# Cross-attention on one core: turned probabilities and y fetched back by quarters of the rows instead of quarters of the keys

## The chip, the cores and the metric

The kernel runs on one NeuronCore of one Trainium2 chip. The metric is the device time of one execution in microseconds (us). A core has a matrix engine (PE, with weight loads shown as PEld), a vector engine (DVE), a scalar engine (ACT), GpSimd (POOL) and a sequencer for transfers (SP). Transfers between HBM and the on-chip memory of 128 partitions are issued on SP's queue here, apart from the loads of the four last text rows and the gathered accumulations, which POOL issues. The profile speaks of the core's 16 DMA engines, which carry out all of them.

## The reference

One layer of cross-attention over `x` (2 x 2048 x 640, f32) with 128 text rows of width 384, 8 heads of 80. The last 4 text rows are the "adapter" rows.

```python
query = hidden_states @ Wq
hs = _mha(query, enc @ Wk, enc @ Wv)              # softmax over 124 text keys
ca_q1 = einsum('btc,th->bch', ca, Wq_ca)[:, indices, :]
ca_hs1 = _mha(ca_q1, residual, residual)          # adapter: the 2048 rows of x are keys and values
ca_hs2 = _mha(ca_hs1 @ Wq, ca @ Wk_ca, ca @ Wv_ca)
out = (hs + ca_hs2) @ Wout + b_out + residual
```

`indices` picks 2048 places out of 384 columns, so only 384 rows of the adapter branch are distinct; the kernel computes these and gathers them for the output rows.

## The kernel before

**Order of work.** A planner (`Desk`, from line 65) replays generators, each of which yields pieces of work with the events that they wait for, the buffers that they need and free, and a rank. It keeps an estimated clock per engine and records, one piece at a time, the one that can start first on its estimate. The order on each engine is therefore fixed when the program is built, and every engine works through its own list in that order. A transfer is recorded by `Desk.dma` (line 263) on SP's list; the number that follows its two sides is only the planner's estimate of its time. When the program runs, an engine waits on semaphores for what its next instruction needs. The transfers of SP go round eight semaphores in turn, so that a transfer is also issued only after the one eight places earlier on SP's list has landed.

**Text branch.** The 2 x 2048 rows are treated as 16 units `m` of two tiles of 128 rows. `text_scores` puts a tile's scores (128 rows x 8 heads x 124 keys) into PSUM, `softmax` turns them into probabilities, and a DVE transposition of 32 x 32 blocks writes them into the single buffer `eb` as `[128, 4, 8, 32]`: partition `32 i + b` is key place `b` of row block `i`, the second index `j` is the quarter of the keys (32 keys each). One transfer of 512 KB carries `eb` to a scratch tensor `kept` in HBM (128 x 4 x 2 x 256 values for both tiles of a unit); `eb` is free when that transfer has landed. This is needed because the block transposition leaves the 32 keys of every quarter on the partitions of their row block, while the product with the values wants all 128 keys on the partitions.

`probabilities` (line 2017) brings a unit back into `pT`, `[128, 4, 2, 8, 32]`: partition `32 j + b` is the key, the second index `i` the row block. It issues four transfers of 256 KB each. There are two `pT` buffers, and the transfers wait for both `kept` transfers of the unit and for the buffer. After that, `residual` (line 2107) issues the loads of the unit's rows of `x` into `x_more` or `last_rows`, `hidden` (line 2144) multiplies `vpad` by `pT` into `ph` (48 matmuls a unit), ACT or DVE copies `ph` to `hs`, and PE multiplies by sums of columns of `Wout` into `po` (`text_out_fast`, line 2171). DVE adds `po` to the loaded rows of `x`, POOL adds the adapter's result by a gathered, accumulating transfer (`add_second`), and SP stores the tile.

**Adapter branch.** For each of two batches `b` and four blocks `sb` of 512 rows, `yz_block` makes `yz` on PE. `y_rows` (line 1609) turns its y part by 32 x 32 blocks on DVE into `yt`, sends it to a scratch tensor in HBM by two transfers, and fetches it back into `y_sb` by four transfers of 128 KB. The z part becomes `zop`; for the second batch it goes to HBM and comes back as `zb`. `s` is the product of `zop` and `cop`, `ea` its exponential on ACT, and `contract` multiplies `ea` by `y_sb[:, sb, g]` into `acc`, for `g` from 0 to 3. The blocks of the second batch overwrite those of the first, so their fetch waits for the first batch's `acc`.

**Queries.** `pq` is made in blocks of 512 rows. What of its split into high and low parts is needed by the scores goes to HBM as `away` and returns as `landing`, which ACT casts to `rests`; the second half of a tile's scores (`sc<-krest,rests`) waits for that.

Of the kernel before, what the change touches and what calls it, by code (L numbers as in the profile page):

```python
# [64 lines left out]
class Desk:  # L65
# [197 lines left out]
    def dma(self, out, in_, us, issue=0.45, more=2.8):  # L263

        self.pin(self.nc.sync.dma_start(out, in_))
        self.spent += issue
        self.channel = max(self.channel, self.now + self.spent) + us
        self.landed = self.channel + more
# [3 lines left out]
def kernel(  # L272
# [29 lines left out]
    R = D2 - P  # L302
# [11 lines left out]
    matmul, transpose, copy, dma = desk.matmul, desk.transpose, desk.copy, desk.dma  # L314
# [94 lines left out]
    y_sb = const.tile([P, NSB, 4, 2, 4, G], F32, name="y_sb")  # L409
# [1119 lines left out]
    def yz_block(b, sb):  # L1529
# [24 lines left out]
        for u in range(2):  # L1554
            yield Do(
                "ACT", lambda u=u: desk.a_activation(yz[:, u, :], pyz[u], AF.Identity, bias=ones),
                [op.at], frees=[(banks, s[u])], marks=[("yz", b, sb, u)],
            )
        yield Fork(y_rows(b, sb), 9)
        away = hbm.tile([P, 2, 512], F32, tag=f"z_{sb}", name=f"z_{b}_{sb}") if b else None  # L1560
        if not b:
# [47 lines left out]
    def y_rows(b, sb):  # L1609

        yz = yz_of[b, sb]
        kept = hbm.tile([P, 4, 2, 4 * G], F32, tag=f"y_{b}_{sb}", name=f"y_{b}_{sb}")
        for u in range(2):

            def turn(z, u=u):
                t = late["pool"].tile([P, 512], F32, tag=f"yt{z[0]}", name=f"yt_{b}_{sb}_{u}")
                desk.v_transpose(
                    t.rearrange("p (a s k) -> p a s k", a=4, s=4),
                    yz[:, u, :].rearrange("p (s a t) -> p a s t", s=4, a=4),
                )  # L1620
                return t

            op = yield Do("DVE", turn, [("yz", b, sb, u), "late"], needs=[(yts, 1)], rank=0.5)

            def away(t=op.value, u=u):
                dma(kept[:, :, u, :], t.rearrange("p (a n) -> p a n", a=4), 1.0)

            yield Do("SP", away, frees=[(yts, op.slots[0][0])], marks=[("y out", b, sb, u)], rank=0.5)
        both = [("y out", b, sb, u) for u in range(2)]
        yield Do(  # L1630
            "NONE", lambda: None, [("zop", b, sb, u, "away") if b else ("zop", b, sb, u) for u in range(2)] + both,
            frees=[(yzs, 0)],
        )
        yield Do("NONE", lambda: None, both + ([("acc done", b - 1, u) for u in range(2)] if b else []))
        by_tokens = kept.rearrange("(g t) a u n -> a t g (u n)", g=4)
        for a in range(4):

            def back(a=a):
                dma(
                    y_sb[R * a : R * (a + 1), sb].rearrange("p g u s k -> p g (u s k)"),  # L1640
                    by_tokens[a], 0.4,
                )

            op = yield Do("SP", back, rank=0.5, marks=[("y", b, sb, a)])

    def adapter(b):

# [369 lines left out]
    def probabilities(m):  # L2017

        yield Do("NONE", lambda: None, [("kept", m, 0), ("kept", m, 1)])
        kept = kept_of[m].rearrange("p j k n -> p j (k n)")  # L2020
        by_keys = kept.rearrange("(i b) j n -> j b i n", i=4)
        op = yield Do(
            "NONE", lambda z: wide("pT", z[0], f"pT_{m}"), needs=[(pTs, 1)], marks=[("back", m)],
        )
        room_of["pT", m] = op.slots[0][0]
        pT = op.value
        for j in range(4):
            op = yield Do(
                "SP",
                lambda: dma(pT[R * j : R * (j + 1)].rearrange("p i k h a -> p i (k h a)"), by_keys[j], 1.1),  # L2030
                [("kept", m, 0), ("kept", m, 1)], rank=0,
            )
        pT_of[m] = pT
        desk.event(("pT", m)).t = op.at.t
        yield from text_out(m)
# [3 lines left out]
    def wide(kind, i, name):  # L2039

        if i == SPARE:
            t = slot(spare[kind], name, [P, 4, 2 * HEADS * R])
            return t.rearrange("p i (k h a) -> p i k h a", k=2, h=HEADS)
        return late["pool"].tile([P, 4, 2, HEADS, R], F32, tag=kind, name=name)
# [92 lines left out]
    def text_out(m):  # L2137

        N = 2 * P
        b = tiles(m)[0][0]  # L2140
        rank = lambda: 30 + m if desk.known(("o2", b)) else 60 + m
        yield from text_out_fast(m, rank)
# [182 lines left out]
    def text(m):  # L2325

        yield Fork(residual(m), 30 + m - 0.5)
        yield Fork(text_scores(m), lambda: m if not any(t is not None for t in qslots.at) else 10 + m)
        yield Fork(probabilities(m), 30 + m)
# [64 lines left out]
```

## Time and profile before

| what | value |
|---|---|
| time, median of 3 runs (range) | 582.21 us (582.02 to 582.29) |
| profiled execution: its own time | 581.8 us |
| profiled execution: span | 580.1 us |
| PE busy | 570.3 us |
| DVE busy | 391.7 us |
| ACT busy | 309.8 us |
| POOL busy | 141.6 us |
| bytes read from HBM, written | 71.23 MB, 40.22 MB |
| transfers `pT<-kept` | 64 of 256 KB |
| transfers `y_sb<-y` | 32 of 128 KB |

Times in the profile are from the start of the span. A row of the list of transfers gives the tile written and the tensor read, the issuing queue, how many, the size of one, and the median time from its issue to its landing, where the trace tells it. In a table of stretches each row is a stretch of time, with the busy time of each engine, the granted clock of PE (1.00 is full), the share of time in which the 16 DMA engines had a packet in hand (their mean; overlapping packets can bring it above 1), and the GB/s moved. The chain of waits is followed back from the last instruction: each piece was released by the piece before it.

### The profile page before, as it was taken

The numbers are of one execution on the slowest core, as the hardware profiler recorded it, in microseconds if no ns is written. First come the engines' busy times: TensorE is split into PE (matmuls) and PEld (weight loads), VectorE is DVE, ScalarE is ACT, GpSimd is POOL, SyncE is SP. The second block draws the span as 40 slices with busy tenths as digits, with TensorE's granted clock in tenths as the row PEclk, the third lists the DMA queues.
The fourth block names the chain that finished last, engine by engine and source line by source line (L and its number), as shares of the span: only waits on it lengthen the run. The fifth ranks groups of instructions, "written<-read, shape, count | busy, mean of one in ns | idle before, by whom it ended". The sixth has DMA issues, their size and how long they took to land.

```text
span 580.1 us, 19105 instructions
## 1 busy us (share of the span) xinstructions
PE 570.3 (98%) x8115; PEld 308.4 (53%) x8115; DVE 391.7 (68%) x645; ACT 309.8 (53%) x869; POOL 141.6 (24%) x200
## 2 busy tenths in 40 slices
PE   9999999999999999999999999999999999999997
PEld 8885334555555545455455445454455545545453
DVE  2446799999999756356999999973455253444443
ACT  2413376686566898689847447277877613002020
POOL 9102112012206411120114326050140312403241
PEclk9999999999999999999999999999999999999999
DMA  8897866979766888234999969999549487799995
GB/s 245 196 263 131 199 94 187 179 201 172 182 184 137 217 157 221 82 113 149 219 284 247 230 152 236 270 227 275 142 105 266 112 211 155 181 263 247 250 249 139
DMA packets 153039, 112.71 MB, mean 194 GB/s; under 512 B 83701, under 2 KB 126581, under 8 KB 152954
## 3 DMA queue, kind: packets, MB, share of 16 engines
q1 hardware_dynamic: 147322, 100.80, 67.5%
q0 software_dynamic: 5632, 10.69, 11.3%
q8 instruction: 64, 1.05, 0.8%
q14 instruction: 21, 0.17, 0.1%
HBM read 71.23 MB, written 40.22 MB: 192 GB/s over the span
## 4 chain that ended last, share of the span: by engine, by line
PE 64%; DVE 16%; DMA 8%; ACT 6%; issue 4%; SPq 1%; DVEq 0%; ACTq 0%
PE po L222 25%; PE pq L222 9%; PE ph L210 6%; DVE mx L245 6%; PE acc L210 5%; PE s L210 4%; PE pq L210 4%; PE sc L210 3%; ACT ea L245 3%; DMA kept<-eb 3%; DMA pT<-kept 2%; ACT p L245 2%; DVE m L245 2%; DVE q L245 2%; DVE eb L245 2%
## 5 line engine op out<-in xcount | busy, mean ns | idle before, releaser
L245 DVE TENSOR_REDUCE mx<-s 128x4 f32<-128x2048 f32 x48 | 109.4, 2280 | 4.1 <-PE s L210 4.1
L245 ACT ACTIVATE ea<-s 128x2048 f32<-128x2048 f32 x48 | 91.0, 1897 | 24.2 <-PE s L210 23.9
L245 ACT ACTIVATE p<-sc,m 128x124 f32<-128x124 f32 x256 | 90.2, 383 | 10.2 <-DVE m L245 9.7
L222 PE MATMUL po<-wout_sums,hs 128*32 128x320 f32 x1024 | 77.3, 433 | 0.0
L222 PE MATMUL po<-wout_sb,hs 128*32 128x320 f32 x960 | 74.2, 433 | 0.7 <-DVE x_more L245 0.7
L222 PE MATMUL pq<-xt,wq_sb 128*32 128x256 f32 (+1 forms) x928 | 66.3, 418 | 0.5 <-DVE mt L245 0.5
L245 DVE TENSOR_TENSOR x_more<-x_more,po 128x320 f32<-128x320 f32 x72 | 34.3, 483 | 45.5 <-PE po L222 45.4
L2129 POOL DMA_INDIRECT x_more<-o,query x18 | 27.9, 1550 | 124.3 <-DVE x_more L245 92.5
L245 ACT ACTIVATION_READ_ACCUMULATOR p<-sc,m 128x1 f32 x256 | 57.8, 226 | 0.0
L245 ACT COPY hs<-ph 128x512 f32<-128x512 f32 (+1 forms) x34 | 18.5, 551 | 65.8 <-PE ph L210 65.2
L222 PEld LDWEIGHTS po<-wout_sums,hs 128*32 128x32 f32 x1024 | 32.9, 110 | 34.1 <-issue 1.8
L210 PE MATMUL acc<-ea,y_sb 128*32 128x384 f32 (+2 forms) x768 | 51.0, 385 | 0.0
L222 PEld LDWEIGHTS po<-wout_sb,hs 128*32 128x32 f32 x960 | 30.4, 110 | 33.1 <-issue 1.5
L245 DVE TENSOR_REDUCE m<-sc 128x4 f32<-128x496 f32 x64 | 40.0, 662 | 10.4 <-PE sc L210 10.4
L245 DVE TENSOR_TENSOR last_rows<-last_rows,po 128x320 f32<-128x320 f32 x56 | 26.7, 481 | 27.9 <-PE po L222 27.5
L210 PE MATMUL ph<-pT,vpad 128*32 128x256 f32 x768 | 45.3, 380 | 0.1
L245 POOL TENSOR_TENSOR p<-p,r 128x992 f32<-128x992 f32 x8 | 14.8, 1846 | 125.0 <-DVE r L245 125.0
L222 PEld LDWEIGHTS pq<-xt,wq_sb 128*32 128x32 f32 x928 | 27.8, 109 | 29.6 <-issue 13.5
L245 DVE STREAM_TRANSPOSE eb<-p 128x1024 f32<-128x1024 f32 x32 | 39.4, 1233 | 5.6 <-DMA kept<-eb 5.5
L210 PEld LDWEIGHTS sc<-kmain,q 64*128 64x128 f32 x512 | 32.1, 187 | 13.7 <-issue 5.5
L210 PE MATMUL sc<-kmain,q 64*128 64x124 f32 x512 | 38.4, 285 | 0.2 <-ACT p L245 0.2
L245 ACT CAST rests<-landing 128x512 fp32r<-128x512 f32 x30 | 18.7, 635 | 36.2 <-PE sc L210 28.0
(216 smaller groups left out, 847.6 us busy)
## 6 DMA issues: line engine op xcount, KB each, us to landing
kept<-eb SPq DMA_DIRECT2D x32, 512.0 KB, 3.8
pT<-kept SPq DMA_DIRECT2D x64, 256.0 KB, 8.2
landing<-away SPq DMA_DIRECT2D x60, 128.0 KB, 4.3
xi<-in_x_dram SPq DMA_DIRECT2D x56, 128.0 KB, 4.6
x_more<-in_x_dram SPq DMA_DIRECT2D x18, 320.0 KB, 6.8
out_dram<-x_more SPq DMA_DIRECT2D x16, 320.0 KB, 6.6
last_rows<-in_x_dram SPq DMA_DIRECT2D x14, 320.0 KB, 7.2
out_dram<-last_rows SPq DMA_DIRECT2D x14, 320.0 KB, 10.0
```

Of the source, the lines that this page charges most:

```text
L210: self.pin(self.nc.tensor.matmul(out, lhsT, rhs, **kw))
L222: self.pin(self.nc.tensor.matmul(out[j : j + 32], lhsT[:, j : j + 32], rhs, **kw))
L245: self.pin(getattr(engine, what)(*args, **kw))
L2129: desk.pin(nc.gpsimd.indirect_dma_start(out=t, out_offset=None, in_=o2_of[b], in_offset=bass.IndirectOffsetOnAxis(ap=query[:, st : st + 1] ...
```

## The change

Both fetches still consist of four transfers of the same size, and each still moves pieces of 2 KB (`pT`) or 1 KB (`y_sb`), 128 pieces a transfer. What one transfer covers is different. Before, transfer `j` (for y: `a`) covered one quarter of the keys: it wrote 32 partitions, four pieces in each. Now transfer `i` (for y: `g`) covers one quarter of the rows: it writes all 128 partitions, one piece in each.

The pattern that a transfer walks, from the outermost index to the innermost, is this:

| | tile side before | HBM side before | tile side after | HBM side after |
|---|---|---|---|---|
| `pT` | 32 x 4 x 512 | 32 x 4 x 512 | 128 x 512 | 4 x 32 x 512 |
| `y_sb` | 32 x 4 x 256 | 32 x 4 x 256 | 128 x 256 | 4 x 32 x 256 |

On the HBM side the outermost index after the change is the quarter of the keys (4 of them) and the next is the key within the quarter (32). The two can't be merged, since a quarter's step in HBM is one piece and a key's step is four (for `pT`).

The order of instructions is the same on every engine, and no buffer and no transfer is added or removed. The planner's estimates and the number of its marks are the same too.

```diff
-        by_tokens = kept.rearrange("(g t) a u n -> a t g (u n)", g=4)
-        for a in range(4):
+        by_tokens = kept.rearrange("(g t) a u n -> g a t (u n)", g=4)
+        for g in range(4):
 
-            def back(a=a):
+            def back(g=g):
                 dma(
-                    y_sb[R * a : R * (a + 1), sb].rearrange("p g u s k -> p g (u s k)"),
-                    by_tokens[a], 0.4,
+                    y_sb[:, sb, g].rearrange("p u s k -> p (u s k)"),
+                    by_tokens[g], 0.4,
                 )
 
-            op = yield Do("SP", back, rank=0.5, marks=[("y", b, sb, a)])
+            op = yield Do("SP", back, rank=0.5, marks=[("y", b, sb, g)])
...
-        by_keys = kept.rearrange("(i b) j n -> j b i n", i=4)
+        by_keys = kept.rearrange("(i b) j n -> i j b n", i=4)
...
-        for j in range(4):
+        rows_of_keys = pT.rearrange("p i k h a -> i p (k h a)")
+        for i in range(4):
             op = yield Do(
                 "SP",
-                lambda: dma(pT[R * j : R * (j + 1)].rearrange("p i k h a -> p i (k h a)"), by_keys[j], 1.1),
+                lambda: dma(rows_of_keys[i], by_keys[i], 1.1),
                 [("kept", m, 0), ("kept", m, 1)], rank=0,
             )
```

`R` is 32. The semaphores on which the `acc` matmuls and the fetches of the second batch's y wait follow the parts of `y_sb` that they touch: before, a matmul for group `g` read something of all four fetches, and a fetch overwrote something of all four groups; now both belong to one `g`.

## The prediction, made before the run

> **What bounds the kernel.** First the page, for each engine's share and the transfers over time; then PE's own waits (sum in us, how many, longest).
>
> ```profile
> span 580.1 us, 19105 instructions
> PE 570.3 (98%) x8115; PEld 308.4 (53%) x8115; DVE 391.7 (68%) x645; ACT 309.8 (53%) x869; POOL 141.6 (24%) x200
> DMA  8897866979766888234999969999549487799995
> ...
> PE po L222 <- DVE x_more L245: 0.7, 2, 0.5
> ...
> PE sc L210 <- ACT p L245: 0.2, 1, 0.2
> ```
>
> PE is busy 570.3 of 580.1 us, so all waits and pauses of PE together are 9.8 us. That is the most that any faster transfer could give back. The other direction has no such limit: the 16 DMA engines are 90% busy or more in many slices from the twentieth on, so what makes transfers dearer there is not obviously hidden. The table by stages says where (the columns after the clock are DMA share and GB/s):
>
> ```profile
> 60.00:193.00 133.00, 131.99 (x1882) 65.58 (x1874) 124.89 (x162) 86.78 (x314) 31.70 (x35) 1.00 0.75 171
> 193.00:275.00 82.00, 80.66 (x1299) 43.32 (x1291) 48.02 (x81) 68.78 (x143) 11.52 (x10) 1.00 0.57 152
> 275.00:306.00 31.00, 29.65 (x410) 15.57 (x414) 30.13 (x39) 19.82 (x77) 3.69 (x2) 1.00 1.03 255
> 306.00:357.00 51.00, 50.29 (x742) 25.93 (x736) 49.87 (x52) 28.81 (x116) 23.14 (x22) 1.00 0.89 210
> 357.00:407.00 50.00, 49.48 (x746) 24.88 (x746) 35.39 (x56) 31.84 (x80) 10.93 (x10) 1.00 0.98 256
> 407.00:505.00 98.00, 97.97 (x1529) 50.74 (x1533) 42.58 (x87) 49.08 (x88) 21.11 (x17) 1.00 0.68 168
> 505.00:530.00 25.00, 25.00 (x400) 12.99 (x396) 10.93 (x24) 3.17 (x7) 8.05 (x6) 1.00 0.98 239
> 530.00:557.00 27.00, 27.00 (x436) 14.20 (x431) 12.64 (x29) 4.55 (x9) 6.46 (x5) 1.00 1.04 254
> ```
>
> From 275 to 407 and from 505 to 557 the DMA engines have no room. The chain of waits shows that PE's list hangs on transfers there with nothing to spare:
>
> ```profile
> 299.74 6.15 DMA zb<-z
> ...
> 307.97 1.87 PE sc L210 x24
> ...
> 316.64 8.04 DMA x_more<-in_x_dram
> 324.69 5.86 DMA pT<-kept
> 330.55 0.87 DVE x_more L245 x2
> ...
> 331.46 3.44 PE po L222 x48
> ...
> 385.40 8.21 DMA pT<-kept
> ...
> 393.67 11.11 DMA kept<-eb
> ...
> 404.88 0.06 DVE eb L245
> ...
> 406.94 1.82 PE po L222 x24
> ```
>
> Three places: `zb` at 306, the rows of `x` at 331, and `kept` at 405, whose landing frees `eb`, for which DVE waits, and behind DVE the additions that free PE's banks.
>
> **The change, part by part.** Nothing moves on any queue, SP's and POOL's included; bytes, pieces and issues are the same, so SP's issue time stays. The second-batch fetches of y now each wait for their own group's `acc` matmuls, where the first used to wait for all: never later, zero. An `acc` matmul needs one fetch instead of four: a gain only if y is late; zero. What is left is the duration of 64 + 32 transfers, and what stands behind them.
>
> *How many engines share a transfer.* The new HBM side has 4 as its outermost count; the tile side has 128. Before, both had 32. If the pieces are dealt to engines by outermost entries, only 4 engines can work on a transfer; if by pieces, 16. The trace of before shows no large transfer of this shape. The nearest rows are the adapter's loads, 4 rows of 1.5 KB, against loads of 16 rows of `Wout`:
>
> ```profile
> wout_sb<-in_L_xattn_Wout_dram SPq DMA_DIRECT2D x8, 40.0 KB, 1.9
> ...
> ca<-in_ctx_dram POOLq DMA_DIRECT2D x32, 6.0 KB, 4.1
> ```
>
> The 4-row load takes 4.1 us for a seventh of the bytes that a 16-row load lands in 1.9 us. It is issued by another queue, so this leans towards "few engines" without settling it. I take 4 engines, because both patterns must be cut at the same places, and an outermost count of 4 offers only 3 cuts.
>
> The Trainium skill, page "DMA: Bandwidth & Descriptors", section "Why a DMA increments its semaphore by 16 and not by 1", gives a rule for this: the engine count is the largest number up to 16 that divides the slowest dimension (other than 1) of both patterns, and the lowest-numbered engines are used. By it these transfers get 4 engines, always the same 4, and the sum below holds; by dealing single pieces they would get 16, the first rival. No row here tests it on a large transfer.
>
> *The price of a unit.* Two stretches, one with `pT` alone (32 partitions at a time), one with 128-partition transfers alone:
>
> ```profile
> DMA packets 274, 0.50 MB, mean 208 GB/s; under 512 B 30, under 2 KB 30, under 8 KB 274
> ...
> DMA packets 681, 0.99 MB, mean 395 GB/s; under 512 B 39, under 2 KB 463, under 8 KB 681
> q1 hardware_dynamic: 681, 0.99, 107.0%
> ```
>
> 16 engines at 395 GB/s are 24.7 GB/s each. A unit of `pT` is 4 x 262 KB = 1.05 MB: before 1.05 MB / 208 GB/s = 5.0 us on all engines; after, on four engines, 1.05 / 98.8 = 10.6 us, which is 5.6 us more on those four. Bounds: 16 engines at 395 GB/s give 2.65 us, 2.4 us less. A y fetch (131 KB) goes from 0.63 us (taking the same 208 GB/s, an estimate) to 1.33 us: 0.7 us more, or 0.3 less.
>
> Nearly all other SP transfers are spread over all engines, so each lands only when the four have done their share. What is issued behind units of `pT` is late with them: the `kept` at 393.67 stands behind two and took 11.1 us, where the median is 3.8.
>
> ```profile
> kept<-eb SPq DMA_DIRECT2D x32, 512.0 KB, 3.8
> ```
>
> So the four engines' extra work is added to the stretch, less the room in it. In all: 16 x 5.6 + 32 x 0.7 = 112 us, the upper end if nothing hides.
>
> ```profile
> y_sb<-y SPq DMA_DIRECT2D x14, 128.0 KB, 4.3
> pT<-kept SPq DMA_DIRECT2D x4, 256.0 KB, 7.2
> ...
> pT<-kept SPq DMA_DIRECT2D x12, 256.0 KB, 8.6
> ...
> pT<-kept SPq DMA_DIRECT2D x16, 256.0 KB, 10.5
> ```
>
> (Issues from 275 to 299.8, that is up to `zb`; from 306 to 331.4; from 355 to 393.7, up to the `kept`.)
>
> - 60 to 275: 16 y fetches, 11.2 us of extra work on the four; the room is 0.25 x 133 + 0.43 x 82 = 68 us. Cover: the fetches are spread singly. I take 1 us, for a `landing` or `kept` caught behind one.
> - 275 to 306: one unit and 14 y fetches before `zb`: 5.6 + 9.8 = 15.4 us. The share is 1.03, no cover, and `zb` has none at 307.97. 15 us.
> - 306 to 357: three units and two y fetches, 18.2 us; room 0.11 x 51 = 5.6 us. The `x` rows at 316.64 stand behind one unit; the third unit is issued by 330.2, lands near 339 at 8.6 us and is used from 352 on (rows below), so it has some 12 us in hand. 5.6 us for the first, and of the rest what the room doesn't take, mostly under the third's lead: 8 us.
> - 357 to 407: four units, 22.4 us, all ahead of the `kept` at 393.67. Share 0.98, but the row above shows 1.07 to be possible: room 0.09 x 50 = 4.5 us. 17 us.
> - 407 to 505: four units, 22.4 us against 0.32 x 98 = 31 us of room; `pT` is fetched a unit ahead. 1 us.
>
> ```profile
> 327.47 2.77 SPq L265 DMA_DIRECT2D pT<-kept  x4
> ...
> 351.41 1.93 PE L210 MATMUL ph<-pT,vpad 128*32 128x256 f32 x32
> ```
>
> - 505 to 557: four units, 22.4 us, shares 0.98 and 1.04. Here only lead time is cover:
>
> ```profile
> 529.91 2.10 SPq L265 DMA_DIRECT2D pT<-kept  x4
> ...
> 532.59 5.80 SPq L265 DMA_DIRECT2D pT<-kept  x4
> ...
> 551.64 5.37 PE L210 MATMUL ph<-pT,vpad 128*32 128x256 f32 x96
> ...
> pT<-kept SPq DMA_DIRECT2D x8, 256.0 KB, 11.1
> ```
>
> The second unit is issued by 538.4 and, at the 11.1 us that is typical from 530 to 557, has landed near 549; it is used half-way through the 96 matmuls, at 554.3. So 11.2 us of delay meet 5 us of lead: some 6 us. I take 5 for each of the two pairs (505 and 530), since the room after 407 lets the first pair start with empty queues: 10 us.
>
> Sum: 1 + 15 + 8 + 17 + 1 + 10 = 52 us. The profiled execution took 581.8 us (span 580.1 and 1.7 around it), 0.4 under the median; 581.8 + 52 = 634.
>
> **The rivals.**
>
> *Sixteen engines, and faster.* All 128 partitions are written at 395 instead of 208 GB/s: a unit needs 2.65 us, and the stretches at 1.03, 0.98 and 1.04 get room. For it: the gap between the two rows just used. The gain is bounded by what PE stands idle while the DMA engines are full: from 275 to 407 it is 1.35 + 0.71 + 0.52 = 2.6 us by the table, of which PE's waits name 0.9 (the additions at 331 and 407, the scores at 308). 581.8 - 2.6 = 579.2 us. It holds from the point where a transfer is dealt out finer than its 4 outermost entries. The Trainium skill, page "DMA: Bandwidth & Descriptors", section "Rules for kernel authors", advises 128 partitions for most bandwidth; the trace agrees so far as 395 against 208 GB/s goes.
>
> *Sixteen engines, and no change.* The 208 GB/s may come from reading pieces 8 KB apart in HBM, which stays. 582 us.
>
> *Four engines, but only the fetches themselves are late.* If other transfers were not held behind them, only the pairs after 505 would fall short, by 11.2 - 5 = 6 us each, less if the first pair's delay gives the second more lead: 8 us in all, `zb` and `kept` untouched. 590 us. Against it: the 11.1 us of that `kept`.
>
> *Nothing hides:* 581.8 + 112 = 694 us, if the four engines bound every stretch; the room from 193 to 275 and from 407 to 505 speaks against it.
>
> **How the numbers follow.** Four engines with most of the delay on PE's path: 0.70, 610 to 670 by itself. Four engines with little of it on the path: 0.14, 584 to 610. More than 670: 0.03. Sixteen engines and faster: 0.07; sixteen and no change: 0.06. The range of 590 to 670 leaves out the sixteen-engine cases, the tail above and the mildest of the second case: 0.2. Faster by over 0.2% 0.07, within 0.2% (about what can be told from no change) 0.06, slower 0.87.
>
> **What would show it.** In the new profile PE's share falls to about 90%, with new waits of PE's `s`, `sc` or `ph` around 300 to 410 and after 520; stretches with `pT` alone move about 100 GB/s instead of 208 with a DMA share near 0.25; `landing`, `kept`, `zb` and the `x` rows land later than before, from 275 on. Wrong on the engine count: `pT` alone near 395 GB/s. Wrong on the queueing: 100 GB/s, but `kept` still lands in 3.8 us. Wrong on cover: late landings, but PE's share stays at 98%.

## The result, and the profile after

| what | before | after |
|---|---|---|
| time, median (range) | 582.25 us (582.02 to 583.54) | 675.40 us (672.88 to 678.18) |
| ratio of after to before, 95% interval | | 1.1592 (1.1546 to 1.1639) |
| profiled execution: time, span | 581.8, 580.1 us | 672.88, 671.1 us |
| mean granted clock of PE | 1.00 | 0.941 |

The changed kernel is 16% slower, 93 us. The direction was forecast; the time lies 41 us above the forecast 634 and 5 us above the end of the range.

The page of the kernel after, its first lines, the clock and the shares of the chain:

```profile
span 671.1 us, 19103 instructions
...
PE 591.5 (88%) x8115; PEld 314.6 (47%) x8115; DVE 392.9 (59%) x645; ACT 309.4 (46%) x869; POOL 141.5 (21%) x200
...
PEclk9999999999999999989699697996999979987979
DMA  8997668876588633545565546846255464674675
...
PE 55%; DMA 20%; DVE 12%; ACT 5%; SPq 3%; issue 3%; DVEq 0%; ACTq 0%
```

The span is 91.0 us longer, and the page splits this in two. PE's busy time rose from 570.3 to 591.5 us for the same 8115 matmuls: 21.2 us. The rest, 69.8 us, is idle time of PE (9.8 us before, 671.1 - 591.5 = 79.6 us now). From the eighteenth slice on the clock row has gaps; before, every slice showed a 9. And where the DMA row stood at 9 in the later half, it now mostly stands between 4 and 6: the kernel waits longest for transfers while the 16 engines together are half idle.

PE's own waits after (sum in us, how many, the longest), largest first:

```profile
PE ph L210 <- DMA pT<-kept: 22.5, 2, 13.2
PE po L222 <- DVE x_more L245: 22.0, 3, 11.8
PE pm L230 <- DVE mt L245: 9.0, 1, 9.0
PE ph L210 <- ACT o L245: 5.3, 1, 5.3
```

Before, the same list has no wait of PE longer than 1.1 us. Only the first row names a changed transfer. What stands behind the second is in the list of all engines, first after, then before:

```profile
DVE eb L245 <- DMA kept<-eb: 42.3, 7, 16.2
...
ACT rests L245 <- DMA landing<-away: 25.4, 3, 16.4
```

```profile
ACT rests L245 <- DMA landing<-away: 8.2, 2, 5.9
...
DVE eb L245 <- DMA kept<-eb: 5.5, 2, 5.0
```

DVE waits for stores of `kept`, that is for transfers that the change didn't touch, and PE's banks wait behind DVE. The chain of waits says the same in order of time (start, length in us):

```profile
286.03 12.38 DMA y_sb<-y
...
300.27 7.75 DMA zb<-z
...
360.29 16.07 DMA kept<-eb
...
445.53 13.93 DMA kept<-eb
...
528.84 11.85 DMA out_dram<-x_more
...
585.77 21.29 DMA pT<-kept
...
622.92 20.67 DMA pT<-kept
```

The `kept` that took 11.11 us on the chain before (at 393.67) is the one at 445.53 and takes 13.93; another, at 360.29, which was not on the chain before, takes 16.07. In the last stages a fetch of `pT` that took 11.1 us takes 21. A table by stages, cut so that each row holds the same matmuls as a stage of before (275 to 306, 306 to 357, 357 to 407, 407 to 505, 505 to 530, 530 to 557); the columns are those of the table in the prediction:

```profile
275.60:321.10 45.50, 34.41 (x411) 17.09 (x415) 30.91 (x39) 19.37 (x75) 3.69 (x2) 0.90 0.54 169
321.10:389.95 68.85, 56.65 (x742) 28.72 (x736) 50.81 (x54) 29.28 (x118) 23.20 (x22) 0.87 0.56 163
389.95:462.16 72.21, 51.48 (x745) 25.48 (x744) 34.80 (x54) 32.01 (x80) 10.85 (x10) 0.86 0.57 172
462.16:569.26 107.10, 101.77 (x1529) 50.83 (x1525) 42.68 (x87) 48.53 (x87) 18.32 (x16) 0.95 0.52 148
569.26:608.02 38.76, 25.56 (x396) 11.93 (x392) 11.85 (x26) 3.36 (x7) 10.94 (x7) 0.88 0.67 164
608.02:647.82 39.80, 30.49 (x433) 15.82 (x429) 11.83 (x26) 4.16 (x8) 6.16 (x4) 0.86 0.60 175
```

Every stage that had a DMA share near 1 now has 0.54 to 0.67. The difference in length to the stage of before, the part of it by which PE was busy for longer, and the rest, which is idle time, all in us:

| stage (times of before) | predicted | longer by | PE busy longer | idle |
|---|---|---|---|---|
| 60 to 275 | 1 | 0.4 | 0.1 | 0.3 |
| 275 to 306 | 15 | 14.5 | 4.8 | 9.7 |
| 306 to 357 | 8 | 17.9 | 6.4 | 11.5 |
| 357 to 407 | 17 | 22.2 | 2.0 | 20.2 |
| 407 to 505 | 1 | 9.1 | 3.8 | 5.3 |
| 505 to 557 | 10 | 26.6 | 4.1 | 22.5 |
| sum | 52 | 90.7 | 21.2 | 69.5 |

The granted clock is not merely lower on average. By the trace's own record of it, it is at 0.50 in ten stretches between 294.7 and 646.3 us and at 1.00 in between. The sum over these ten (us of time, then busy time of each engine):

```profile
sum 78.50, PE 41.13 PEld 20.14 DVE 26.57 ACT 10.08 POOL 9.43; mean PE 4.11 PEld 2.01 DVE 2.66 ACT 1.01 POOL 0.94
```

PE was busy for 41.1 us at half clock. At full clock that work would take about half as long (in the one-stall kernel below, 48 matmuls take 5.34 us at half clock and 2.77 at full), so 20.6 of the 21.2 us of added busy time are the clock.

Finally a stretch in which nearly all that flows is `pT` (the transfers of 626 to 628 us; packets, MB, share of the 16 engines):

```profile
DMA packets 102, 0.20 MB, mean 101 GB/s; under 512 B 4, under 2 KB 4, under 8 KB 102
...
q1 hardware_dynamic: 102, 0.20, 26.1%
```

101 GB/s at a quarter of the engines, where the kernel before had 208 GB/s at 95% (437 to 439.4 us, the first stretch in the prediction). The start and length of each packet in the trace say the same directly: in these 2 us four packets are under way at any moment, or five for the instant in which one follows another.

### The profile page after: what moved, and what is told of

The parts are those of the page before. It is cut to its first block, busy times and chain, and to the rows that moved or that the text cites. A ratio compares the mean times of both kernels' runs of the same rounds, so it can differ in the third digit from the quotient of the medians.

```text
span 671.1 us, 19103 instructions
## 1 busy us (share of the span) xinstructions
PE 591.5 (88%) x8115; PEld 314.6 (47%) x8115; DVE 392.9 (59%) x645; ACT 309.4 (46%) x869; POOL 141.5 (21%) x200
## 4 chain that ended last, share of the span: by engine, by line
PE 55%; DMA 20%; DVE 12%; ACT 5%; SPq 3%; issue 3%; DVEq 0%; ACTq 0%
PE po L222 15%; PE pq L222 11%; DMA pT<-kept 6%; PE ph L210 5%; DMA kept<-eb 5%; PE acc L210 5%; DVE mx L245 4%; PE sc L210 4%; PE s L210 4%; DMA out_dram<-x_more 4%; SPq L265 3%; PE pq L210 3%; ACT ea L245 3%; DMA zb<-z 2%; DMA y_sb<-y 2%
## 5 line engine op out<-in xcount | busy, mean ns | idle before, releaser
L222 PE MATMUL po<-wout_sums,hs 128*32 128x320 f32 x1024 | 79.9, 444 | 10.1 <-DVE x_more L245 10.1
L210 PE MATMUL ph<-pT,vpad 128*32 128x256 f32 x768 | 51.6, 417 | 27.9 <-DMA pT<-kept 22.5
L222 PE MATMUL pq<-xt,wq_sb 128*32 128x256 f32 (+1 forms) x928 | 67.8, 426 | 1.1 <-ACT p L245 0.7
L245 DVE STREAM_TRANSPOSE eb<-p 128x1024 f32<-128x1024 f32 x32 | 39.5, 1233 | 42.5 <-DMA kept<-eb 42.3
L245 DVE TENSOR_TENSOR x_more<-x_more,po 128x320 f32<-128x320 f32 x72 | 34.3, 482 | 47.3 <-PE po L222 47.2
L245 ACT CAST rests<-landing 128x512 fp32r<-128x512 f32 x30 | 18.7, 633 | 67.5 <-PE sc L210 42.1
L210 PEld LDWEIGHTS ph<-pT,vpad 128*32 128x32 f32 x768 | 25.7, 119 | 49.8 <-issue 30.0
L245 DVE TENSOR_REDUCE m<-sc 128x4 f32<-128x496 f32 x64 | 40.0, 661 | 11.5 <-PE sc L210 11.4
L245 DVE TENSOR_TENSOR hs<-hs 128x256 f32<-128x256 f32 x42 | 17.6, 424 | 49.5 <-ACT hs L245 44.8
L245 DVE TENSOR_TENSOR last_rows<-last_rows,po 128x320 f32<-128x320 f32 x56 | 26.6, 482 | 28.7 <-PE po L222 28.5
L210 PE MATMUL sc<-kmain,q 64*128 64x124 f32 x512 | 40.2, 291 | 3.2 <-ACT p L245 1.6
```

Of the source, the lines that this page charges most:

```text
L210: self.pin(self.nc.tensor.matmul(out, lhsT, rhs, **kw))
L222: self.pin(self.nc.tensor.matmul(out[j : j + 32], lhsT[:, j : j + 32], rhs, **kw))
L245: self.pin(getattr(engine, what)(*args, **kw))
```

## The experiments

Unless its expectation says so, no kernel here leaves out or changes a part of the computation.

### Each half of the change by itself

The two hunks of the diff, one at a time, on the kernel before: first the fetch of the probabilities alone, then that of y alone.

> The probabilities' fetch as in the changed kernel, the y fetch as before. Theory A (the HBM side's outermost count of 4 puts each transfer on four engines, and everything issued behind it waits): the units of pT are 16 x 5.6 of the 112 us of extra engine work, so most of the loss stays; the part of it up to 325 us, where 16 y fetches stand in front of zb, shrinks from 17 us to some 6. 655 to 668 us. Rival Y (the y fetches before zb start the delay and the rest is inherited): under 620 us.

> The y fetch as in the changed kernel, the probabilities' fetch as before. Theory A: 16 fetches between 278 and 305 with 0.7 us of extra work each, of which 14 before zb: 8 to 14 us more than before, so 590 to 597 us, all of it lost between 285 and 330 us, and no loss at the first batch's y before 275 us. Rival Y: over 620 us. If all of it hides under the DMA engines' room: 582 us.

Measured: the probabilities alone 664.24 us, ratio 1.1388 (1.1360 to 1.1415); y alone 596.57 us, ratio 1.0231 (1.0196 to 1.0265). Both lie in what was expected. Against 582.57 us for the kernel before in the same session that is 81.7 and 14.0 us, together 95.7 where both changes together cost 93: the halves add up, nearly. The page of the kernel with y alone:

```profile
span 595.4 us, 19103 instructions
...
PE 577.7 (97%) x8115; PEld 310.9 (52%) x8115; DVE 392.6 (66%) x645; ACT 309.9 (52%) x869; POOL 141.6 (24%) x200
...
PEclk9999999999999999999978999999999999999999
```

All its loss comes between 296 and 335 us, where the fetches of the second batch's y go out in a row; the sixteen fetches of the first batch, spread singly before 275 us, cost nothing. Of the 15.3 us by which this span is longer, 7.4 are busy time of PE (577.7 - 570.3), again with a gap in the clock row.

### Two engines, and sixteen

If the number of engines is what counts, a fetch cut so that its HBM side has two outer entries should be dearer still, and one with 128 outer entries on both sides should cost nothing. First, on the kernel after, each fetch of `pT` in two halves of 64 partitions:

```diff
-                lambda: dma(rows_of_keys[i], by_keys[i], 1.1),
+                lambda: [
+                    dma(rows_of_keys[i][64 * J : 64 * J + 64], by_keys[i][2 * J : 2 * J + 2], 0.55, issue=0.225)
+                    for J in range(2)
+                ],
```

> The changed kernel, but each fetch of pT is cut into two of 128 KB for 64 partitions each, so that the HBM side is 2 x 32 x 512. Theory A: two engines a transfer, and the same two each time: 49 GB/s with pT alone, 21 us a unit, 340 us of work on two engines from 275 us on beside some 140 us of the other transfers' shares; 275 + 480 and more, so 760 to 850 us. Rival B: the time stays at 660 to 680 us, since the pieces and the partitions are the same.

Measured: 843.5 us (one run), within what was expected. A stretch of its trace with `pT` alone, from 653 to 658.5 us:

```profile
DMA packets 135, 0.27 MB, mean 49 GB/s; under 512 B 6, under 2 KB 6, under 8 KB 135
...
q1 hardware_dynamic: 135, 0.27, 13.1%
```

Half the rate and half the share of the kernel after. From 653 to 656 us two packets are under way, now and then three or four, and never fewer.

Second, on the kernel before, keys put in another order over the partitions of `pT`: partition `4 b + j` instead of `32 j + b`. Each fetch then takes one row block to all 128 partitions, and the HBM side is 128 x 512 as the tile side is. `vpad`, whose rows must follow, is made from a copy of the text with permuted rows (two copies by POOL).

```diff
-        by_keys = kept.rearrange("(i b) j n -> j b i n", i=4)
+        by_keys = kept.rearrange("(i b) j n -> i (b j) n", i=4)
...
-        for j in range(4):
+        rows_of_keys = pT.rearrange("p i k h a -> i p (k h a)")
+        for i in range(4):
...
-                lambda: dma(pT[R * j : R * (j + 1)].rearrange("p i k h a -> p i (k h a)"), by_keys[j], 1.1),
+                lambda: dma(rows_of_keys[i], by_keys[i], 1.1),
...
+                lambda b=b: desk.g_tensor_copy(
+                    ctxP[:, b].rearrange("p c (t j) -> p c t j", j=4),
+                    ctxT[:, :, b, :].rearrange("p c (j t) -> p c t j", j=4),
+                ),
```

> The kernel before, but the keys stand on the partitions of pT as 4 x key-in-quarter + quarter, so that quarter and key merge on the HBM side and a fetch of pT is 128 x 512 on both sides; the values' rows are put in the same order by two copies of 128 x 384 on POOL early on, and no DVE transposition is changed. y is fetched as before. If the 21 us that the every-fourth version lost come from its slower DVE transpositions (2.12 against 1.23 us), and sixteen engines with 128 partitions are as fast as its packets showed (84 ns a 2 KB packet): 579 to 582 us. If a fetch over 128 partitions costs something by itself: 590 us or more.

Measured: 581.57 us (12 runs) against 582.56 us (17 runs), ratio 0.9984 (0.9974 to 0.9993). The page of this kernel, SP's queue; in the kernel before the same row says 67.5%:

```profile
q1 hardware_dynamic: 147322, 100.80, 61.7%
```

The transfers of 536 to 539 us, when `pT` and a few loads and stores of rows over 128 partitions flow:

```profile
DMA packets 629, 1.21 MB, mean 403 GB/s; under 512 B 69, under 2 KB 69, under 8 KB 629
...
q1 hardware_dynamic: 629, 1.21, 104.8%
```

In this stretch 16 packets or a few more are under way, and never fewer. So filling 128 partitions is not what is slow: with 16 engines it goes at 403 GB/s, where the fetch of before, over 32 partitions and with pieces 8 KB apart in HBM, had 208 GB/s, and the engines' whole work on this queue falls from 67.5% to 61.7% of the span. Two, four and sixteen engines give 49, 101 and up to 403 GB/s: 25 GB/s for each engine in all three. And it is worth 1 us only, because PE was busy 98% of the time already. This version is 0.16% faster than the kernel before, which counts here as no change.

### Sixteen engines by another block transposition

Another way to give the changed fetch 128 outer entries: DVE's transposition takes every fourth key (for y, every fourth row) into a block, so that keys come to lie in HBM in the order in which the 128 partitions want them. On the kernel after:

```diff
-            desk.v_transpose(eb, e.rearrange("p h (j b) -> p j h b", j=4))
+            desk.v_transpose(eb, e.rearrange("p h (b j) -> p j h b", j=4))
...
-        by_keys = kept.rearrange("(i b) j n -> i j b n", i=4)
+        by_keys = kept.rearrange("(i b) j n -> i (b j) n", i=4)
...
-                    yz[:, u, :].rearrange("p (s a t) -> p a s t", s=4, a=4),
+                    yz[:, u, :].rearrange("p (s t a) -> p a s t", s=4, a=4),
...
-        by_tokens = kept.rearrange("(g t) a u n -> g a t (u n)", g=4)
+        by_tokens = kept.rearrange("(g t) a u n -> g (t a) (u n)", g=4)
```

> The changed kernel, with the blocks of the two DVE transpositions taken over every fourth key (token) instead of 32 neighbours. Then the quarter and the key merge on the HBM side into one index of 128, and each fetch is 128 x 512 (128 x 256 for y) on both sides; it still covers a quarter of the rows and writes all 128 partitions, with the same number of instructions in the same order. Theory A: the whole loss is gone; a unit of pT takes some 2.7 us instead of 5.0 before; 578 to 582 us, at best 2.6 us under the kernel before. Rival B (writing all 128 partitions by one transfer, or reading neighbouring pieces, is what is slow): 640 us or more.

Measured: 603.39 us, ratio 1.0350 (1.0331 to 1.0369). 72 of the 93 us are gone, but 21 remain, and neither theory had foreseen that. The group of the transpositions of the probabilities (busy time in us, mean ns of one), of this kernel and then of the kernel before:

```profile
L245 DVE STREAM_TRANSPOSE eb<-p 128x1024 f32<-128x1024 f32 x32 | 67.8, 2119 | 1.5 <-DMA kept<-eb 1.4
```

```profile
L245 DVE STREAM_TRANSPOSE eb<-p 128x1024 f32<-128x1024 f32 x32 | 39.4, 1233 | 5.6 <-DMA kept<-eb 5.5
```

The instructions of the tile `yt` (shortest, median and longest in ns), in the same order, and PE's largest wait of this kernel:

```profile
L245 DVE STREAM_TRANSPOSE yt<-yz x16: 1079/1157/1248, 65.5 to 271.4; 128x512 f32<-128x512 f32 x16
```

```profile
L245 DVE STREAM_TRANSPOSE yt<-yz x16: 669/700/714, 64.6 to 253.6; 128x512 f32<-128x512 f32 x16
```

```profile
PE s L210 <- DVE mx L245: 8.8, 12, 1.8
```

The transposition that reads with a stride of four elements takes 2.12 us instead of 1.23, and that of y 1.16 instead of 0.70: 28.4 + 7.3 = 35.7 us more on DVE. PE's waits for DVE's maxima all end before 345 us, and most of the loss falls there: the first `ph` product starts 19.3 us later than in the kernel before (335.4 against 316.1 us), the last 22.6 us later (579.0 against 556.4). The stalls behind transfers are gone, so this run agrees with the previous two on the transfers. That the slower transpositions cost the 21 us follows from the version above, which has 16 engines for `pT` without them and loses nothing; PE's waits for the maxima name only 8.8 us. The y fetch with 128 outer entries was not run without them.

### The last four units alone

The stage from 505 to 557 us was sized at 10 us and lost 26.6. Either it inherits lateness from the stages ahead, or the term itself was too small. On the kernel before, only the four units whose fetches go out from 505 us on get the changed fetch:

```diff
+        late_four = m in (12, 13, 8, 15)
...
-                lambda: dma(pT[R * j : R * (j + 1)].rearrange("p i k h a -> p i (k h a)"), by_keys[j], 1.1),
+                lambda: dma(rows_of_keys[j], by_rows[j], 1.1) if late_four else dma(
+                    pT[R * j : R * (j + 1)].rearrange("p i k h a -> p i (k h a)"), by_keys[j], 1.1
+                ),
```

> The kernel before, with the changed fetch only for the last four units of pT (those issued from 505 us on); y as before. Theory A with the trace of the changed kernel: PE's stalls at the two pairs of units, 13.2 and 9.3 us there, do not depend on the backlog of the stages before, so 22 us of stall and some 4 us of matmuls at half clock come back: 604 to 610 us. By the prediction's own term for this stage: 592 us. If the stalls were inherited from the stages before: 582 to 587 us.

Measured: 607.24 us, ratio 1.0436 (1.0419 to 1.0453), 24.7 us over the kernel before, as the first of the three expectations has it. The stage costs this much with nothing late ahead of it. The timeline of this kernel, PE's two stalls (in brackets):

```profile
540.39 4.97 PE L210 MATMUL ph<-pT,vpad 128*32 128x256 f32 x48 [10.65 <-DMA pT<-kept]
576.03 4.22 PE L210 MATMUL ph<-pT,vpad 128*32 128x256 f32 x48 [8.70 <-DMA pT<-kept]
```

The prediction had 5 to 6 us for each of these stalls. What makes up the rest may be seen in POOL's queue, which carries the gathered accumulations (packets, MB, share of the engines). First this kernel, from 505 us until the pair has landed at 540.4 us, and the part of that from 524 us on; below it the kernel before, from 505 to 524 us:

```profile
q0 software_dynamic: 977, 2.21, 39.3%
...
q0 software_dynamic: 567, 1.29, 47.3%
```

```profile
q0 software_dynamic: 402, 0.90, 30.3%
```

POOL issues four gathers between 521 and 530 us in both kernels. In the kernel before, the pair has mostly landed by then. In this one it is still on its four engines, and the gathers take 47.3% of all engines, 7.8 us of each.

### The same without four gathers

That reading was tried: the previous kernel, with the four gathers of 521 to 530 us replaced by copies of four elements.

```diff
+        gathers.append((b, st))
+        if len(gathers) in (21, 22, 23, 24):
+            desk.pin(nc.gpsimd.tensor_copy(t[:, :4], t[:, :4]))
+        else:
             desk.pin(nc.gpsimd.indirect_dma_start(
```

> Edit: the kernel with the changed fetch for the last four units only (607.24 us, first stall of PE 10.65 us, second 8.70 us), and besides the four gathered, accumulating transfers that POOL issues at 521 to 530 us are left out (POOL copies four elements onto themselves in their place), so four tiles of the output lack the adapter's part. What is to be told apart: why the pair of units fetched from 505 us on came 10.65 us late and not the 6 us that the prediction's sum gives. Theory A: staying longer on their four engines, the fetches run into the gathers of 521 to 530, which in the kernel before come when the pair has mostly landed. POOL's queue took 47.3% of the engines from 524 to 540.4 us, 7.8 us of each engine, and 0.90 MB before against 2.21 MB in the span of the pair. Without the four gathers the first stall should fall to 3 to 6 us, the second stay at 7 to 9 us, the time come to 597 to 602 us. Rival B: the gathers are served beside the fetches at no cost, and the lateness is the four engines' own work and SP's held-up issues: first stall 10 to 11 us, time 605 to 608 us.

Measured: 601.15 us (599.40 to 602.17), ratio 1.0327 (1.0297 to 1.0357). That is 19.2 us over the kernel before in the same session (581.91 us), where it was 24.7 with the gathers. Its timeline:

```profile
533.43 5.35 PE L210 MATMUL ph<-pT,vpad 128*32 128x256 f32 x48 [3.97 <-DMA pT<-kept]
570.46 4.12 PE L210 MATMUL ph<-pT,vpad 128*32 128x256 f32 x48 [9.51 <-DMA pT<-kept]
```

The first stall falls from 10.65 to 3.97 us, the second, whose gathers were left in, does not. SP issued the pair's last fetch at the same time in both kernels (518.95 and 518.51 us); by the chain it then took 21.31 us to land with the gathers and 14.78 without. The gathers more than account for the first stall's excess over the prediction's 5 to 6 us. The second stall came out a little above the expected 7 to 9 us; that its excess has the same cause was not tried.

### One stall without a changed transfer

The busy time of PE rises by 21.2 us, and the clock has gaps. Either the clock falls because PE stands still, or because of the transfers themselves. In the kernel before, with no transfer changed, ACT copies the last unit's `pT` six times onto itself ahead of its product, so that PE must wait once:

```diff
+                if m == UNITS - 1 and c0 == 0:
+                    for _ in range(6):
+                        desk.pin(nc.scalar.copy(pT_of[m], pT_of[m]))
```

> The kernel before, with six copies of the last unit's pT onto itself on ACT between its landing and its ph matmuls, so that PE stands still once, near 554 us, for some 9 to 11 us. No transfer is changed. Theory C (PE's granted clock falls to a half while PE stands still and stays there for some microseconds after): PE's busy time grows by 2 to 5 us, and the time by 11 to 16 us, 593 to 598 us. Rival D (the longer matmuls of the changed kernel come from its transfers, through the on-chip memory): PE's busy time stays at 570.3 us, and the time grows by the stall alone, 591 to 593 us.

Measured: 596.24 us, ratio 1.0229 (1.0205 to 1.0254), within what theory C gives. The page of this kernel:

```profile
PE 574.5 (96%) x8115; PEld 308.2 (52%) x8115; DVE 391.4 (66%) x645; ACT 320.7 (54%) x875; POOL 141.4 (24%) x200
```

The timeline of PE around the stall:

```profile
553.05 2.77 PE L210 MATMUL ph<-pT,vpad 128*32 128x256 f32 x48
...
567.25 5.34 PE L210 MATMUL ph<-pT,vpad 128*32 128x256 f32 x48 [11.42 <-ACT pT L2182]
```

Two windows (the clock is the third number from the end):

```profile
551.00:570.00 19.00, 7.58 (x112) 3.73 (x108) 2.81 (x7) 13.31 (x10) 6.35 (x5) 0.72 0.83 202
570.00:580.00 10.00, 10.00 (x140) 4.41 (x133) 4.00 (x9) 0.96 (x2) 0.00 (x0) 0.85 0.01 2
```

A stall of 11.42 us costs 4.2 us of busy time on top (574.5 - 570.3), with the transfers as before. After the stall 48 matmuls of one kind take 5.34 us, before it 2.77. PE's standing still is enough to lower the clock; no changed transfer is needed.

The Trainium skill, page "TensorE: Matmul & The Clock Gate", section "Part 1: The HAM clock gate (the "warmup" mystery)", states this: after an idle window of about 3.4 us PE's clock is halved, and it is whole again after about as long a busy window, in windows that run freely. The runs agree: taken at 0.50, the lowered clock of the two windows above makes (0.28 x 19 + 0.15 x 10) / 0.5 = 13.6 us, which is four such windows; by the trace's record of the clock it is at 0.50 from 559.4 to 573.0 us, beginning 3.6 us after PE fell idle (553.05 + 2.77 = 555.8) and with its last 5.8 us after work had begun again at 567.25.

## Why the prediction failed, step by step

**The engine count: right.** Four engines from the outermost count of 4 was the choice between two readings; 101 GB/s at 26.1% where `pT` flows alone is the number given beforehand (about 100 GB/s, share near 0.25), and the series of 2, 4 and 16 engines confirms it from both sides. The rule of the Trainium skill, page "DMA: Bandwidth & Descriptors", section "Why a DMA increments its semaphore by 16 and not by 1", gave this number, and gives 2 and 16 for the two experiments' shapes; the packets under way (4, 2 and 16) agree with all three. Which four engines they are, no view here shows.

**The queueing: right.** Late are above all transfers that were not changed: `kept` at 13.93 and 16.07 us, `landing`, `zb`, the store `out_dram` at 11.85. The rival by which only the fetches themselves would be late (590 us) falls with that, as do both rivals with sixteen engines. That of a gain by sixteen engines is right as to the rate (403 GB/s), but only for a fetch with 128 outer entries on both sides, and its gain of at most 2.6 us measured 1.0.

**Which stages lose: nearly right.** 60 to 275 us cost 0.4 us (1 predicted), 275 to 306 us cost 14.5 (15 predicted; y alone, 14.0). From 306 on every term was too low.

**The sum: wrong, by two causes.** The first is a term that it didn't have. It counted a stall as its own length; the matmuls after a stall run at half the clock for some us. That is 21.2 us of the 91, 30% on top of the idle time; 20.6 of it lie in the stretches at half clock. The stage from 275 to 306 us came out right only because its idle part was smaller (9.7 us) than the predicted 15 and the clock made up for it.

The second is the cover: 52 us of idle time predicted, 69.5 measured. The step that failed most is the one for 505 to 557 us, "11.2 us of delay meet 5 us of lead". It took the landing time of before and added the extra work of two units. But a fetch that stays longer on its engines meets other work there that used to come later: the four gathers of 521 to 530 us. They account for some 6.7 us of the first stall (10.65 - 3.97). The same kind of step, room in the mean share of a stage taken as cover, failed from 407 to 505 us: 31 us of room for 22.4 us of work, yet 9.1 us lost. The timeline of SP after shows why:

```profile
520.35 4.94 SPq L265 DMA_DIRECT2D pT<-kept  x4
...
528.84 1.99 SPq L265 DMA_DIRECT2D out_dram<-x_more  x1
540.71 0.33 SPq L265 DMA_DIRECT2D x_more<-in_x_dram  x1
541.09 0.47 SPq L265 DMA_DIRECT2D o<-o  x1
```

One unit of `pT`, 10.6 us by the prediction's price, stands just ahead of a store; the store lands at 540.69, only then is the next load into its buffer issued, behind that load the transfer of `o`, and PE waits 5.3 us for what ACT makes of `o`. Room elsewhere in the 98 us doesn't help. From 306 to 357 us, 11.5 us of idle time against 8, and from 357 to 407, 20.2 against 17, the error is 3 us each; no run divided these further, and what makes them up is open. So is the excess of the second stall after 505 us, 8.7 to 9.5 us where the prediction had 5 to 6.

One more term was put at nothing and wasn't nothing: "SP's issue time stays". The median issue of `pT<-kept` rose from 428 to 602 ns and the longest from 1.2 to 6.7 us (last section), and SP's part of the chain from 1% to 3%. What this alone cost, no run separates.

## What to carry to other kernels

Before changing the shape of a transfer, look at the outermost counts of both of its sides: here 128 against 4 left 4 of 16 engines, 101 GB/s where 16 reach 403, and transfers queued behind it were late as well; putting the rows in an order in which both sides count 128 gave all engines back. When a delay is costed, add what a stall does to PE's clock (here 21 us on 70 us of stalls), and ask which transfers of other queues the longer transfer will now meet; the mean DMA share of a long stage is no cover for a wait inside it. And when a faster transfer is on offer, look first at the idle time of the engine that bounds: at 98% busy, 403 instead of 208 GB/s was worth 1 us.

## What the runs showed of the hardware that was not expected

- A block transposition on DVE (f32) that reads its source with a stride of four elements takes 1.65 to 1.72 times as long: 2119 against 1233 ns for 128 x 1024, 1157 against 700 ns for 128 x 512.
- The fetch that fills 32 partitions goes at 208 GB/s, the reordered one that fills 128 at 403 GB/s, both with all 16 engines; a packet of 2 KB took 144 ns (median over the run) in the first kernel and 84 ns in the second. The second also reads neighbouring pieces where the first reads pieces 8 KB apart. With 4 engines and 128 partitions, pieces 8 KB apart took 84 ns too, which speaks for the partitions, but no run separates the two at 16 engines.
- SP's issues become longer when its transfers back up. The times of one issue of `pT<-kept` (ns, shortest, median, longest), of the kernel after and then of the one with two engines:

```profile
L265 SPq DMA_DIRECT2D pT<-kept x64: 507/602/6747, 275.3 to 622.9; - x64
```

```profile
L265 SPq DMA_DIRECT2D pT<-kept x128: 482/2446/9420, 277.0 to 799.5; - x128
```

In the kernel before the median was 428 ns and the longest 1175 ns. With two engines the median issue takes 2.4 us; a fetch of half the size at 49 GB/s lasts 131 KB / 49 GB/s = 2.7 us, so SP issues about as fast as the two engines work them off. Whatever stands behind on SP's list is held up with it.
